# Gates of a graph network by seven half-array products over pairs of batches

## The chip, the core and the metric

The kernel runs on one core of a Trainium2 chip. The metric is the device time of one execution in microseconds (us). PE is TensorE, DVE VectorE, ACT ScalarE, POOL GpSimd; SP is SyncE, which here only issues DMA transfers.

## The reference

There are 16 batches of 1024 nodes with 128 features, and one 1024 x 1024 matrix `adj`, all float32. Layer 0 is `x = layernorm(x + adj (x W) + b)`. Layer 1 is a gated recurrence of five steps, with `adj` for both of its matrices, then again `layernorm(x + h)`:

```
m  = adj @ h;  av = concat([m, m])
u3 = h @ u3_w.T + u3_b
z  = sigmoid(av @ w3_w.T + w3_b + u3)
r  = sigmoid(av @ w4_w.T + w4_b + u3)
hv = tanh(av @ w5_w.T + w5_b + (r * h) @ u5_w.T + u5_b)
h  = (1 - z) * h + z * hv
```

As both halves of `av` are equal, the kernel adds the two halves of each `w` once and works with 128 x 128 matrices.

## The kernel before

**Work units.** Batches go in quads: four quads, five steps each, 20 steps. A tile called `rows` holds nodes on partitions (the form that the aggregation needs), a tile `hid` holds features on partitions (the form that the gates need). `agg` holds the aggregate of the quad, features on partitions, one batch to a slice.

**The aggregation** (`aggregate`, L417) is a two-level Strassen scheme in Winograd's form: seven products of half the size in the place of eight, on two levels. The seven outer products are computed in four chains, "12", "3", "67" and "54", each with an inner scheme of seven products (`chain`, L358). The right operands are sums of blocks of `rows`: `outer_sums` (L342) writes the outer ones to `tsum`, `inner_sums` (L315) the inner ones to `inner`. Chain 12 reads batches 0 and 1 of the quad only; chain 3 reads the second column half of batches 2 and 3; chains 67 and 54 read `tsum`, which takes both halves of all. Each product ends in a PSUM bank (`pa`, `pb`, `pc`), and a copy on ACT or an addition on DVE takes it on. The adjacency matrix's sums are made once.

**The gates.** The work of a step is cut into eight units, a batch and a half of its nodes (512 columns) each. A unit has five full products: `u3` (`gate_first`, L498), `w4` added to it for r (`gate_r`, L515), `w3` added to an ACT copy of it for z (`gate_z`, L531), then `w5` and `u5` in one bank (`update_products`, L539). `update_half` (L548) is tanh on ACT and a subtraction, a product and an addition on DVE. PE's order is written out by hand with `in_order`, so that a unit's `u3` stands well ahead of its other products. The first three units' `u3` products (`gates_begin`) stand between two steps.

**Back to rows.** A finished batch (for batch 3 each half) is turned in blocks of 32 x 32 on DVE (`turn_rows`, L577), written to a scratch tensor in DRAM by one transfer and read back by four (`fetch_rows`, L590), all in SP's queue in program order. The last step of a quad writes to `closing` instead, and the next quad's rows come from `saved`, which holds layer 0's result. The closing of a finished quad (`close`, `layernorm`) is spread over the next quad's steps. The very last step has an order of its own (`ending`).

**Order.** Where the text says nothing, a planner with its own costs picks the order of an engine's instructions; `keep_in_program_order` (also `in_order`) pins an instruction behind the one before it on its engine, `issue_after` queues one behind another, and hooks place work between the products of a chain.

## Time and profile before

| | |
|---|---|
| median of 3 runs | 1768.46 us (1768.37 to 1768.57) |
| the profiled execution, in all | 1769.02 us |
| its span, first to last instruction | 1766.9 us |
| busy: PE, DVE, ACT, POOL | 99%, 74%, 45%, 6% of the span |
| from one step to the next (u3 products at 448.57 and 525.21) | 76.64 us |

A profile is of one execution. The span lies between the first and the last instruction; the rest is around it. In the groups of instructions a line gives the source line, engine, operation, result and operands, shape and count, then the busy time, the mean of one in ns, and the idle time of the engine before them. In the timeline a line gives start and length in us; a float32 product is two PE instructions, whose recorded lengths overlap, so that what a product takes of PE is read from start to start. Of the DMA issues, the last column is the median time from issue to landing.

### The profile page before, as it was taken

The page shows a single profiled execution, that of the slowest core. Times are in us where ns is not written, and L with a number is a line of the kernel's source. Part 1 is how long each engine was busy: PE and PEld are TensorE (multiplying, and loading weights), DVE is VectorE, ACT ScalarE, POOL GpSimd, SP SyncE. Part 2 cuts the span into 40 slices and gives each one's busy share as a digit, 9 for nine tenths or more (in the row PEclk, how much of TensorE's full clock was granted, in tenths as well). Part 3 has the DMA queues.
Part 4 walks back from the last instruction along what each step waited for, and adds up shares of the span by engine and source line. Part 5 has one row for each costly group of instructions (what it writes and reads, how often), then busy time and mean ns, then how long its engine had stood idle before and what let it go on. Part 6 is the DMA issues. An engine that isn't in the chain of part 4 may idle for free.

```text
span 1766.9 us, 19951 instructions
## 1 busy us (share of the span) xinstructions
PE 1755.7 (99%) x6709; PEld 1265.8 (72%) x6709; DVE 1301.9 (74%) x2286; ACT 800.0 (45%) x1424; POOL 103.3 (6%) x152
## 2 busy tenths in 40 slices
PE   9999999999999999999999999999999999999998
PEld 8988885766858577685867758586675857668584
DVE  7977777676766847777778667777778577777778
ACT  4355565334353434435354452535445353443537
POOL 1202220000000000000000000000000000000004
PEclk9999999999999999999999999999999999999999
DMA  8144354051423505143351424324243241514232
GB/s 276 49 143 144 120 137 107 20 119 26 94 60 72 143 12 133 46 120 68 87 131 56 112 57 99 85 71 119 55 113 99 57 93 27 131 25 107 60 84 95
DMA packets 405332, 161.34 MB, mean 91 GB/s; under 512 B 388336, under 2 KB 389488, under 8 KB 405232
## 3 DMA queue, kind: packets, MB, share of 16 engines
q1 hardware_dynamic: 402960, 153.01, 34.3%
q0 software_dynamic: 1696, 5.24, 1.1%
q10 hardware_dynamic: 576, 1.84, 0.3%
q8 instruction: 53, 0.87, 0.2%
q14 instruction: 47, 0.39, 0.1%
HBM read 93.98 MB, written 65.01 MB: 90 GB/s over the span
## 4 chain that ended last, share of the span: by engine, by line
PE 98%; DMA 1%; DVE 0%; POOL 0%; ACT 0%; issue 0%; POOLq 0%; SPq 0%; DVEq 0%; ACTq 0%
PE pb L398 25%; PE pc L398 14%; PE pa L398 14%; PE pu L519 8%; PE ph L542 8%; PE pu L501 8%; PE ph L543 8%; PE seeded L534 8%; PE pc_x L398 3%; PE pa_x L398 3%; PE seeded L475 2%; DMA hid<-in_adj_dram 1%; DMA agg<-in_adj_dram 0%; PE pt L633 0%; PE pt_end L836 0%; POOL rstd L265 0%
## 5 line engine op out<-in xcount | busy, mean ns | idle before, releaser
L398 PE MATMUL pb<-e,inner 128*128 128x256 f32 x864 | 206.2, 379 | 0.2 <-ACT pb L382 0.2
L558 DVE TENSOR_TENSOR tsum<-tsum,hid 128x512 f32<-128x512 f32 x158 | 108.7, 688 | 106.4 <-ACT tsum L553 106.3
L553 ACT ACTIVATE tsum<-ph,bh 128x512 f32<-128x512 f32 x158 | 108.5, 687 | 164.6 <-PE ph L543 164.5
L398 PEld LDWEIGHTS pb<-e,inner 128*128 128x128 f32 x864 | 167.7, 194 | 19.2 <-ACT pb L382 0.6
L519 PE MATMUL pu<-agg,w_t 128*128 128x512 f32 x320 | 163.7, 593 | 0.0
L542 PE MATMUL ph<-agg,w_t 128*128 128x512 f32 x320 | 163.4, 592 | 0.0
L543 PE MATMUL ph<-tsum,u_t 128*128 128x512 f32 x320 | 163.4, 592 | 0.0
L534 PE MATMUL seeded<-agg,w_t 128*128 128x512 f32 x320 | 163.4, 592 | 0.0
L501 PE MATMUL pu<-hid,u_t 128*128 128x512 f32 x320 | 157.0, 592 | 0.0
L522 ACT ACTIVATE tsum<-pu,br 128x512 f32<-128x512 f32 x160 | 110.1, 688 | 85.6 <-PE pu L519 85.6
L398 PE MATMUL pb<-s,inner 128*128 128x256 f32 x576 | 148.5, 380 | 0.0
L398 PE MATMUL pb<-a,inner 128*128 128x256 f32 x576 | 143.9, 379 | 0.0
L529 DVE TENSOR_TENSOR tsum<-tsum,hid 128x512 f32<-128x512 f32 x160 | 110.1, 688 | 37.9 <-ACT tsum L522 37.9
L398 PE MATMUL pc<-e,inner 128*128 128x256 f32 x560 | 133.9, 379 | 0.0
L398 PEld LDWEIGHTS pb<-s,inner 128*128 128x128 f32 x576 | 110.5, 194 | 24.8 <-issue 10.4
L537 ACT ACTIVATE tsum<-seeded,bz 128x512 f32<-128x512 f32 x160 | 110.0, 688 | 29.3 <-PE seeded L534 29.3
L398 PEld LDWEIGHTS pb<-a,inner 128*128 128x128 f32 x576 | 111.9, 194 | 12.4
L398 PEld LDWEIGHTS pc<-e,inner 128*128 128x128 f32 x560 | 109.2, 195 | 12.8 <-PE pu L501 0.7
L543 PEld LDWEIGHTS ph<-tsum,u_t 128*128 128x128 f32 x320 | 60.8, 190 | 76.5 <-issue 59.6
L542 PEld LDWEIGHTS ph<-agg,w_t 128*128 128x128 f32 x320 | 60.6, 190 | 75.1 <-issue 74.4
L501 PEld LDWEIGHTS pu<-hid,u_t 128*128 128x128 f32 x320 | 60.8, 190 | 73.5 <-issue 72.2
L559 DVE TENSOR_TENSOR tsum<-tsum 128x512 f32<-128x512 f32 x158 | 109.1, 691 | 4.9
(192 smaller groups left out, 2854.2 us busy)
## 6 DMA issues: line engine op xcount, KB each, us to landing
turned<-ypad SPq DMA_DIRECT2D x48, 512.0 KB, 3.8
rows<-turned SPq DMA_DIRECT2D x192, 128.0 KB, 2.9
hvs<-saved SPq DMA_DIRECT2D x24, 512.0 KB, 4.1
rows<-saved SPq DMA_DIRECT2D x20, 512.0 KB, 3.7
hid<-hidden SPq DMA_DIRECT2D x64, 128.0 KB, 3.4
turned<-ypad SPq DMA_DIRECT2D x32, 256.0 KB, 2.9
rows<-turned SPq DMA_DIRECT2D x128, 64.0 KB, 2.1
hidden<-ypad SPq DMA_DIRECT2D x12, 512.0 KB, 4.1
```

Of the source, the lines that this page charges most:

```text
L398: product = nc.tensor.matmul(bank_of[a][:, ts(o, QT)], chunk(a, o, c), left[n][a][:, c, :], start=(a in (1, 5) and o == 0 and c == 0), sto ...
L501: in_order(nc.tensor.matmul(pu, w_t["u3"], hid[:, k, ts(h, HALF)], start=True, stop=True, skip_group_check=True))
L519: in_order(nc.tensor.matmul(pu, w_t["w4"], agg[:, k, cols], start=False, stop=True, skip_group_check=True))
L522: pin(nc.scalar.activation(rh[:, cols], pu, AF.Sigmoid, bias=br))
L529: pin(nc.vector.tensor_mul(rh[:, cols], rh[:, cols], hid[:, k, cols]))
L534: in_order(nc.tensor.matmul(pz, w_t["w3"], agg[:, k, cols], start=False, stop=True, skip_group_check=True))
L537: pin(nc.scalar.activation(z_of[k % 2][:, cols], pz, AF.Sigmoid, bias=bz))
L542: in_order(nc.tensor.matmul(ph, w_t["w5"], agg[:, k, cols], start=True, stop=False))
L543: in_order(nc.tensor.matmul(ph, w_t["u5"], rh_of[k % 2][:, cols], start=False, stop=True))
L553: pin(nc.scalar.activation(hv, ph, AF.Tanh, bias=bh))
L558: pinned(nc.vector.tensor_sub(hv, hv, hid[:, k, cols]))
L559: pinned(nc.vector.tensor_mul(hv, hv, z_of[k % 2][:, cols]))
```

## The change

For all steps but the very last, z and r of a pair of batches are computed as one 2 x 2 block product, [r; z] = [w4; w3] times the aggregate: the blocks of the left are w4 and w3 cut at 64 input features, those of the right are the aggregate cut at 64 features and at half of the nodes. Winograd's form takes seven block products for the eight. Each block product contracts over 64 partitions, and two batches lie side by side: batch e of the pair on partitions 64e to 64e + 63 of `agg`, in a bank of its own. For that, `rows` is kept by pairs: slice 2p + f holds feature half f of both batches of pair p, so that the aggregation gives `agg` in that form. Other parts:

- `w5` is applied as two half products over 64 partitions (`carry`); `u3` and `u5` stay full products over one batch. `u3` is applied to the first half of the nodes and to the difference of the halves (`steps_along`, on POOL), which seeds the banks of the scheme.
- The scheme's right sums are made on DVE for pair 0 and on POOL for pair 1 (`gate_sums`); its running sums are kept in two banks, with ACT copies and DVE additions in between (`gate_product`).
- The subtraction in the update moves from DVE to POOL (`update`).
- Order of a step: gates of pair 0, its u5 products and update, its turning and fetching; seeds and gates of pair 1, its u5 products and update; the next step's chain 12 follows at once. Pair 1's two halves are turned and fetched one after the other, second half of the nodes first.
- Turning writes two transfers of 64 partitions where it was one of 128; both slices of a pair wait for both batches.
- The rows of a new quad are loaded by eight transfers with pieces of 256 bytes (`load_pairs`) in the place of four.
- Weights are kept in `split`, each cut at 64 features and doubled over both partition halves; `whole_weights` puts whole ones together again for the very last step. Room for this comes out of `e12`; two left blocks are first put in `hvs` and copied to their place (`settle_left_12`).

```diff
-            tc.keep_in_program_order(nc.tensor.transpose(pt[:, :P], raw[:, :D], ident))
-            nc.vector.tensor_copy(w_t[name], pt[:, :P])
...
+            for f in range(2):
+                tc.keep_in_program_order(
+                    nc.tensor.transpose(pt[:, ts(f, P)], raw[:, ts(f, P)], ident)
+                )
+            i = SPLIT[name]
+            nc.vector.tensor_copy(
+                split[:, i : i + 2], pt[:, : 2 * P].rearrange("p (f d) -> p f d", f=2)
+            )
+        left_sums(*(split[:, i] for i in (0, 1, 2, 3, 6, 7, 8, 9)))
...
+        sums = gate_sums(0, nc.vector) if pairs else iter(())
         for dst, a, b in ((0, p7, p4), (1, p7, p4), (2, p7, p5), (3, p7, p5)):
             cols = ts(dst % 2, HALF)
             nc.vector.tensor_add(agg[:, dst, HALF:], a[:, cols], b[:, cols])
-            if dst >= 2:
+            if dst == 0:
+                next(sums, None)
+            elif dst == 1:
+                deque(sums, 0)
+            else:
                 nc.vector.tensor_add(agg[:, dst, :HALF], agg[:, dst, :HALF], p5[:, cols])
+        if pairs:
+            deque(gate_sums(1, nc.gpsimd), 0)
...
+    def steps_along(p):
+        for e in range(2):
+            h = hid[:, 2 * p + e]
+            nc.gpsimd.tensor_sub(steps_of_h[:, 2 * p + e], h[:, side(p, 1)], h[:, side(p, 0)])
+
+    def seed_pair(tag, p, role):
+        for e, t in enumerate(take(tag, p, role)):
+            k = 2 * p + e
+            h = hid[:, k, side(p, 0)] if role == "pa" else steps_of_h[:, k]
+            in_order(nc.tensor.matmul(
+                t, w_t["u3"], h, start=True, stop=True, skip_group_check=True
+            ))
...
+    def gate_product(tag, p, a):
+        n1, n2 = side(p, 0), side(p, 1)
+        right = {1: agg[:, 2 * p, n1], 2: agg[:, 2 * p + 1, n1], 3: agg[:, 2 * p + 1, n2]}
+        right.update({a: gate_right[p][:, i] for i, a in enumerate((5, 6, 7, 4))})
+        role = {1: "pa", 2: "pa", 5: "pc", 3: "pc"}.get(a, "pb")
+        for e in range(2):
+            at = ts(e, 64)
+            in_order(nc.tensor.matmul(
+                held[p, role][e], gate_left[a][at], right[a][at], start=False, stop=True,
+                skip_group_check=True,
+            ))
+        if a == 1:
+            take(tag, p, "pb")
+        for e in range(2):
+            pa, pb_, pc = (held[p, i][e] for i in ("pa", "pb", "pc"))
+            z, r = z_to[p][e], r_to[p][e]
+            if a == 1:
+                nc.scalar.copy(pb_, pa)
+            elif a == 5:
+                nc.scalar.copy(z[:, n2], pc)
+            elif a == 6:
+                nc.scalar.copy(r[:, n2], pb_)
+            elif a == 2:
+                nc.scalar.activation(r[:, n1], pa, AF.Sigmoid, bias=br)
+                times_h(p, e, n1)
+            elif a == 3:
+                nc.vector.tensor_add(r[:, n2], pc, r[:, n2])
+                nc.scalar.activation(r[:, n2], r[:, n2], AF.Sigmoid, bias=br)
+                times_h(p, e, n2)
+            elif a == 7:
+                nc.vector.tensor_add(z[:, n2], pb_, z[:, n2])
+                nc.scalar.activation(z[:, n2], z[:, n2], AF.Sigmoid, bias=bz)
+            else:
+                nc.scalar.activation(z[:, n1], pb_, AF.Sigmoid, bias=bz)
+
+    def carry(tag, p, j):
+        to = take(tag, p, f"ph{j}")
+        for f in range(2):
+            for e in range(2):
+                at = ts(e, 64)
+                in_order(nc.tensor.matmul(
+                    to[e], split[at, SPLIT["w5"] + f], agg[at, 2 * p + f, side(p, j)],
+                    start=(f == 0), stop=True, skip_group_check=True,
+                ))
+
+    def gates_of_pair(tag, p):
+        for a in (1, "n1", 2, 5, 6, 3, 7, "n2", 4):
+            if a in ("n1", "n2"):
+                carry(tag, p, int(a[1]) - 1)
+            else:
+                gate_product(tag, p, a)
...
+    def update(p, j, e, put=lambda op: op):
+        cols, k = side(p, j), 2 * p + e
+        hv = rh_of[e][:, cols]
+        nc.scalar.activation(hv, held[p, f"ph{j}"][e], AF.Tanh, bias=bh)
+        nc.gpsimd.tensor_sub(hv, hv, hid[:, k, cols])
+        put(nc.vector.tensor_mul(hv, hv, z_to[p][e][:, cols]))
+        put(nc.vector.tensor_add(hid[:, k, cols], hid[:, k, cols], hv))
...
+        if paired:
+            p, e = divmod(k, 2)
+            moves = [(between(2 * p + f, h)[:, ts(e, 64)], t[ts(f, 64)]) for f in range(2)]
+        else:
+            moves = [(between(k, h) if to is None else to, t)]
+        for to, t in moves:
+            tc.keep_in_program_order(nc.sync.dma_start(to.rearrange("g p x -> p g x"), t))
...
+    def load_pairs(q):
+        for p in range(2):
+            for f in range(2):
+                dst = rows[:, 2 * p + f].rearrange("p (c e x) -> p c e x", c=C, e=2)
+                for e in range(2):
+                    src = saved[q * QUAD + 2 * p + e].rearrange("p (c f x) -> p c f x", c=C, f=2)
+                    nc.sync.dma_start(dst[:, :, e], src[:, :, f])
...
-            for u in range(3, 8):
-                gate_first(tag, u, (u - 3) % 3)
-                step_update(u - 3, (u - 2) % 3)
-                gate_r(u - 1)
-                gate_z(u - 1)
...
-            gates_begin(then, 2 if q == NQ - 1 and s == STEPS - 2 else 3)
...
+            hooks[54][5] = [call(steps_along, 0), call(steps_along, 1)]
+            hooks[54][3, (0,)] = [call(seed_pair, tag, 0, "pa")]
+            hooks[54][4] = [call(seed_pair, tag, 0, "pc")]
+            aggregate(tag, rows, hooks, s > 0, True)
...
+            gates_of_pair(tag, 0)
+            for j in range(2):
+                reset_products(0, j)
+                for e in range(2):
+                    update(0, j, e)
+            for k in range(2):
...
+                    turn_rows(k, None, None, not final)
             if not last:
-                fetch_rows(3, 1)
-                fetch_rows(3, 0)
+                for k in range(2):
+                    fetch_rows(k)
+            seed_pair(tag, 1, "pa")
+            seed_pair(tag, 1, "pc")
+            gates_of_pair(tag, 1)
...
+                sums = first_sums(rows)
+                for j in range(2):
+                    reset_products(1, j)
+                in_order(next(sums))
+                for j, h in enumerate(SIDES[1]):
+                    for e in range(2):
+                        update(1, j, e, in_order)
+                    in_order(next(sums))
+                    for k in (2, 3):
+                        in_order(turn_rows(k, h, None, not final))
+                    for k in (2, 3):
+                        fetch_rows(k, h)
+                in_order(next(sums))
```

## The prediction

> **What bounds the kernel now.** I read the page first. Its chain of work is nearly all PE, and the clock row is 9 in every slice.

> ```profile
> span 1766.9 us, 19951 instructions
> PE 1755.7 (99%) x6709; PEld 1265.8 (72%) x6709; DVE 1301.9 (74%) x2286; ACT 800.0 (45%) x1424; POOL 103.3 (6%) x152
> PE 98%; DMA 1%; DVE 0%; POOL 0%; ACT 0%; issue 0%; POOLq 0%; SPq 0%; DVEq 0%; ACTq 0%
> ```

> PE never waits, so anything taken off PE is gained, and any wait put in front of PE is lost. Then the chain of work in order of time, for the period of a step:

> ```profile
> 448.57 2.58 PE pu L501 x6
> 525.21 2.58 PE pu L501 x6
> ```

> Each line is the three u3 products that open a step (two instructions each): one 512-column product takes 2.58/3 = 0.86 us of PE, and a step 525.21 - 448.57 = 76.64 us. That is 40 gate products (40 x 0.86 = 34.4) plus 98 aggregation products of 256 columns at 0.43. Last the timeline between two steps, engine by engine, because the change rebuilds this stretch:

> ```profile
> 525.05 2.74 PE L501 MATMUL pu<-hid,u_t 128*128 128x512 f32 x6
> 527.62 1.89 PE L398 MATMUL pa<-a,rows 128*128 128x256 f32 x8
> 539.71 1.03 PE L398 MATMUL pa<-s,rows 128*128 128x256 f32 x4
> 544.89 0.59 PE L398 MATMUL pa<-s,tsum 128*128 128x256 f32 x2
> ...
> 531.90 0.71 DVE L581 STREAM_TRANSPOSE ypad<-hid 128x512 f32<-128x512 f32 x1
> 541.51 1.22 DVE L348 TENSOR_TENSOR tsum<-tsum,rows 128x1024 f32<-128x1024 f32 x1
> ...
> 532.64 0.38 SPq L585 DMA_DIRECT2D turned<-ypad  x1
> 533.12 4.08 SPq L596 DMA_DIRECT2D rows<-turned  x8
> ```

> The last gate product ends at 525.05. Chain 12 (batches 0 and 1 only) begins at 527.62, chain 3 (batches 2 and 3, second half) at 539.71, chain 67 (tsum, from both halves of batches 2 and 3) at 544.89. The last transpose is at 531.9, SP's last eight fetches end at 537.2, and the sums that chain 67 reads (L348) end at 542.7: **2.2 us ahead of need**. The price of a transfer is in the page's DMA issues:

> ```profile
> turned<-ypad SPq DMA_DIRECT2D x32, 256.0 KB, 2.9
> rows<-turned SPq DMA_DIRECT2D x128, 64.0 KB, 2.1
> ```

> SP needs 4.08/8 = 0.51 us to issue a fetch and 0.38 plus a gap, 0.42, a write.

> [...] every product of before uses 128 rows, and PE never idles. [...] two L529 took 1.34 us from 1750.08, no longer than elsewhere, under POOL's L814 (1.61 us from 1750.95). So I price POOL's 512-wide subtraction at L814's mean, 1608 ns, with no lock.

> **The change, part by part** (19 steps; the very last keeps the old gates).

> 1. *PE's products.* Per step, 16 products by w4 and w3 become 7 per pair of batches, two half-array products in the place of one: 14 x 0.86. The w5 products become twice as many halves in the same 8 places; u3 and u5 stay 8 and 8. Saved: 2 x 0.86 = 1.72 us a step, **32.7 us** in 19. The halves are not shown in before: at best 0.86 a place, at worst 1.72 (the rival below). I take 0.86. Each pair enters and leaves the half-array mode once; a drain is unknown, between 0 and one half-product's 0.43, and I take 0.1: 0.4 a step.

> 2. *Gate phase, pair 0.* ACT's copies go from 8 to 12 a step (about 0.58 each), tanh and sigmoids stay 24. DVE keeps 32 (8 additions of r and z come, 8 subtractions go to POOL) and gets four sums, L455's 0.60 us apart. From 0.9 us after chain 54's product 4 (its copy), DVE has eleven aggregate operations and sums, then eight of r and z: 0.9 + 19 x 0.60 = 12.3 us. The seventh product, which needs the last z addition off its bank, is due at 0.86 + 0.1 + 10 x 0.86 = 9.6. Late: **2.8 us**. Before, L529 had idle time here, and only ACT's sigmoid emptied a bank. *Pair 1*: products 3 and 7 wait for two sigmoids and four copies in ACT's queue (2 x 0.69 + 4 x 0.5 after product 2, against 3 x 0.86 of PE): about 0.7; the seventh waits again for the z addition behind r's: about 0.8. With the drains **4.7 us a step**; bounds 0.4 (another order of DVE's queue) and 8.

> 3. *Rows of pair 0.* Counted from the end of product 4: POOL's four sums for pair 1 run 7.5 to 14.0, its four subtractions 15.0 to 21.4, multiplication and addition (1.44) to 22.9, transpose (1.25) to 24.1; writes land at about 27.7, eight fetches (0.52 each, 2.9 to land) at 34.3. Pair 1's last product ends at 34.8 (22 half places 18.9, 12 full 10.3, the waits above 4.7, 0.9 for chain 54's rest). So chain 12's rows, well ahead before, are just in time: I take 0.8 us late, bounds 0 and 3.

> 4. *Rows of pair 1: the deciding step.* Let T be the end of the last product, where chain 12 starts; the three u3 products (2.58 us) that used to stand between are now in chain 54. Batches 2 and 3 are now both unfinished at T, in two halves, with all their turns behind them. First half: tanh of both by T - 0.8, POOL to T + 1.5, DVE's product and addition to 3.0, the pinned sum to 3.6, two transposes to 4.9. Each transpose is now two writes: the last starts at 5.3 and lands at 7.8 (2.5, below the 2.9 of 256 KB). SP then issues eight fetches, to 12.0; they land by 13.6. The second half's transposes are long done (9.6), but its writes stand behind those fetches in SP's order: 12.0 to 13.7, landed 15.8; eight fetches to 20.0, landed 21.6; tsum's two operations 1.22 each: **24.0**. Chain 67 is due at 12.1 + 6.05 = **18.15**. PE waits 5.9 us. Chain 3's earlier wait and chain 12's (its sums stand behind the updates on DVE) lie inside that and are not added. With step 3's 0.8 and the pinned sum behind it: **6.9 us**, bounds 2 and 10. It falls in the 16 steps in which rows go on to another step; the three that change quads take rows loaded early and pay only part 2.

> 5. *Once, or hidden.* Eight 256 KB loads instead of four of 512 KB lie behind a whole gate phase, except at the first quad; six small transposes instead of three, their copies and sums, the two copies that settle the left blocks, six ACT copies at the last hand-over: 1.5 us together, bounds 0 and 6. If the gate phase stopped covering the loads it would cost up to 4 us at each of three changes.

> Sum: 16 x (6.9 + 4.7 - 1.72) = 158; 3 x (4.7 - 1.72) = 9; 1.5. The profiled execution took 1769.0 (span 1766.9 and 2.1 around it), 0.5 over the median of the runs shown: 1769.0 + 168.5 - 0.5 = **1937 us**. [...]

> **Rivals.**
> - *The waits are covered: faster.* If DVE's queue serves bank-emptying additions first and the second half's rows come by T + 18, only part 1 is left: 1769 - 32.7 + 7.6 of drains = 1744. It decides at a boundary wait under 32.7/16 = 2.0 us a step with an unhindered gate phase. For it speak PE's lack of any wait before; against it the slack of 2.2, while SP gets six more writes (2.5), four more fetches (2.1) and one more landing (2.5) in a row. Chance 0.09.
> - *The halves take turns.* Then 22 places a step cost 0.86 more: 19 x (18.9 - 1.72) = 327, the gate phase's waits vanish, the boundary's stay at 5.9 x 16 = 94: 2190. Nothing in before speaks on it[...]. Chance 0.10.
> - *Only the boundary counts*, at 4 us, the gate phase near 1.5: 16 x (5.5 - 1.7) = 60, so 1829; 1790 to 1870. Chance 0.18.
> - My forecast: 0.62, by itself 1870 to 2060. Within 0.2% of before, which is about what a measurement of this kernel can tell from no change: 0.01.

> The range 1790 to 2070 takes in the forecast and the third rival and leaves out the other cases, 0.20. Faster 0.09, same 0.01, slower 0.90.

> **What would show it.** PE's busy share falls to about 90%; waits of PE's loads for tsum (L347, L348) appear, 5 to 8 us, some 16 times; SP shows 4 writes, 8 fetches, 4 writes, 8 fetches in the boundary; POOL is busy about 590 us (19 x 16 x 1.61 and before's 103); DVE about 1355, ACT about 850; two half products start 0.43 apart and a pair's place is 0.86. Wrong I am if PE's waits are under 2 us a step, or if the seven products take 1.72 each.

## The result, and the profile after

The changed kernel takes **2204.43 us** (median of 4 runs, 2202.84 to 2210.68) against 1768.41 before: a ratio of 1.2472 (95% interval 1.2448 to 1.2497). Slower, as predicted, but by 436 us where 168 were forecast, and above the range.

The page, with the clock row of its slices:

```profile
span 2208.9 us, 22400 instructions
PE 1967.1 (89%) x7472; PEld 1330.7 (60%) x7472; DVE 1487.9 (67%) x2388; ACT 821.2 (37%) x1508; POOL 587.4 (27%) x456
PEclk9999989999999999999998999998999999989999
```

PE is busy for longer than before (1755.7) with less to do, and the clock row has eights now. PE's waits (engine, line, tile, what ended the wait: total us, times, longest):

```profile
PE pa L430 <- DVE tsum L380: 71.0, 16, 6.1
PE pb L668 <- DVE tsum L691: 51.0, 28, 6.5
PE pb L430 <- DVE inner L350: 32.5, 16, 2.6
PE pc L430 <- DVE inner L349: 28.5, 24, 2.0
PE pa L430 <- DMA rows<-turned: 11.1, 10, 1.6
```

In this kernel L430 is the aggregation product, L668 the half-products of a gate product; L380 makes `tsum`, L349 and L350 are inner sums, L691 is the z addition. The first line is chain 67 at the boundary, 16 times, as predicted. The second is the gate phase of pair 0. The third is chain 12 waiting for its own sums; the fourth is the same in 14 cases and in 10 chain 3 waiting for its.

To see where 436 us went I split PE's time, from its first product to its last, in four. **Work** is the number of products times their start-to-start distance at full clock (0.43 us for an instruction of 512 columns over 128 rows, from 2.58 us for six in the kernel before; 0.216 for 256, from 1.73 us for eight there; half of 0.43 for one of two halves that run side by side, from 1.72 us for eight below). **Idle** is time in which no product runs. **Clock** is busy time multiplied by the share of the clock that was not granted in it. **Rest** is what remains. All four are worked out from the trace of the profiled execution (2210.68 us for the changed kernel); only the runs below test what they mean.

| kernel | work | idle | clock | rest |
|---|---|---|---|---|
| before | 1750.5 | 2.8 | 0.0 | 3.5 |
| changed | 1718.2 | 270.7 | 126.9 | 83.4 |

The idle time is 73.5 us at chain 67 by this count, 67.5 at the inner sums of chain 12 (53.7) and chain 3 (13.8), 69.3 at the z additions (56.5 of pair 0, 12.8 of pair 1), 11.8 at landing rows (nearly all at chain 3), and smaller waits.

Now one step, whose chain 12 starts at T = 612.73. First PE in the gate phase before it (timeline: start, length, engine, line; then the idle time ahead in brackets):

```profile
572.67 0.59 PE L430 MATMUL pc<-e,tsum 128*128 128x256 f32 x2
573.19 1.13 PE L668 MATMUL pa<-agg,split 64*128 64x512 f32 x4
574.15 1.88 PE L701 MATMUL ph<-agg,split 64*128 64x512 f32 x8
575.87 1.02 PE L668 MATMUL pa<-agg,split 64*128 64x512 f32 x4
...
584.65 3.75 PE L668 MATMUL pb<-first,split 64*128 64x512 f32 x4 [1.63 <-DVE tsum L691]
588.32 5.50 PE L715 MATMUL ph<-tsum,u_t 128*128 128x512 f32 x8
593.67 1.88 PE L653 MATMUL seeded<-hid,u_t 128*128 128x512 f32 x4
```

Eight half-array instructions (L701) take 575.87 - 574.15 = 1.72 us: 0.86 for a place of two half-products. So the halves run side by side here. But after a wait, eight full-array instructions (L715) take 593.67 - 588.32 = 5.35 us instead of 3.44. The table of stretches shows why; its columns after the stretch are its length, each engine's busy time and count (PE, PE's loads, DVE, ACT, POOL), then PE's granted clock, the DMA share and GB/s:

```profile
566.20:573.19 6.99, 6.99 (x25) 4.47 (x23) 0.83 (x2) 0.59 (x1) 0.00 (x0) 1.00 0.00 0
573.19:593.67 20.48, 18.66 (x54) 7.52 (x54) 14.02 (x21) 10.33 (x17) 10.01 (x6) 0.83 0.01 1
629.14:641.50 12.36, 5.60 (x25) 4.42 (x23) 3.89 (x6) 2.06 (x5) 0.00 (x0) 0.93 0.58 134
641.50:653.00 11.50, 11.27 (x41) 9.77 (x42) 11.50 (x14) 2.70 (x5) 3.02 (x2) 0.78 0.20 46
```

What goes ahead of such a stretch can be counted in the changed kernel's trace. I cut its time at full clock into pieces of that grid, each ending 0.15 us before a point of it (the first 40 us are left out), and counted in each, from the recorded lengths, the share in which PE's array was in use, a half-array product that runs alone as half. Of 553 pieces 52 have half the clock behind them, with shares of at most 0.48; the 501 others have at least 0.46. Ahead of 585.2 the share was 0.41, though PE stood still for only about 1.6 us: a half ran alone beside the wait. Ahead of 619.3 it was 0.50, and the clock stayed. This is a count in one trace, which no run was made to test.

Then the boundary: SP's queue, and on DVE what it serves:

```profile
620.37 2.63 SPq L748 DMA_DIRECT2D turned<-ypad  x4
624.28 4.17 SPq L757 DMA_DIRECT2D rows<-turned  x8
628.55 2.65 SPq L748 DMA_DIRECT2D turned<-ypad  x4
632.48 4.73 SPq L757 DMA_DIRECT2D rows<-turned  x8
```

```profile
614.29 1.09 DVE L349 TENSOR_TENSOR inner<-rows 128x512 f32<-128x512 f32 x1 [6.21 <-DMA rows<-turned]
615.31 1.75 DVE L725 TENSOR_TENSOR tsum<-tsum,agg 128x512 f32<-128x512 f32 x1
...
639.10 1.23 DVE L379 TENSOR_TENSOR tsum<-rows 128x1024 f32<-128x1024 f32 x1 [7.07 <-DMA rows<-turned]
640.36 1.23 DVE L380 TENSOR_TENSOR tsum<-tsum,rows 128x1024 f32<-128x1024 f32 x1
```

Four writes, eight fetches, four writes, eight fetches: the predicted row. Pair 0's rows come at 614.29, T + 1.6, and the first of chain 12's sums (L349), pinned ahead of pair 1's update, holds DVE's product L725 back until then; and that product takes 1.75 us where such a product took 0.69 before.

### The profile page after: what moved, and what is told of

Read it like the earlier page. It is cut to its first block, busy times and chain, and to the rows that moved or that the text cites. A ratio compares the mean times of both kernels' runs of the same rounds, so it can differ in the third digit from the quotient of the medians.

```text
span 2208.9 us, 22400 instructions
## 1 busy us (share of the span) xinstructions
PE 1967.1 (89%) x7472; PEld 1330.7 (60%) x7472; DVE 1487.9 (67%) x2388; ACT 821.2 (37%) x1508; POOL 587.4 (27%) x456
## 5 line engine op out<-in xcount | busy, mean ns | idle before, releaser
L724 POOL TENSOR_TENSOR tsum<-tsum,hid 128x512 f32<-128x512 f32 x152 | 218.0, 1458 | 376.1 <-ACT tsum L723 375.8
L647 POOL TENSOR_TENSOR inner<-hid 128x512 f32<-128x512 f32 x76 | 116.6, 1538 | 630.5 <-PE pc L430 516.4
L430 PE MATMUL pb<-e,inner 128*128 128x256 f32 x672 | 177.4, 408 | 36.0 <-DVE inner L350 32.5
L430 PE MATMUL pb<-a,inner 128*128 128x256 f32 x760 | 189.8, 383 | 11.9 <-DVE first L418 8.5
L430 PEld LDWEIGHTS pb<-e,inner 128*128 128x128 f32 x672 | 139.1, 209 | 60.8 <-issue 14.2
L430 PE MATMUL pc<-e,inner 128*128 128x256 f32 x560 | 146.2, 403 | 28.7 <-DVE inner L349 28.5
L430 PEld LDWEIGHTS pb<-a,inner 128*128 128x128 f32 x760 | 147.2, 195 | 33.2 <-DVE first L418 9.7
L430 PE MATMUL pb<-s,inner 128*128 128x256 f32 x576 | 162.6, 408 | 4.4 <-DVE rows L418 3.0
L725 DVE TENSOR_TENSOR tsum<-tsum 128x512 f32<-128x512 f32 x76 | 91.0, 1217 | 111.7 <-POOL tsum L724 111.7
L430 PE MATMUL pa<-s,tsum 128*128 128x256 f32 x320 | 97.4, 422 | 71.0 <-DVE tsum L380 71.0
L668 PE MATMUL pb<-first,split 64*128 64x512 f32 x228 | 110.0, 720 | 51.4 <-DVE tsum L691 51.0
L430 PEld LDWEIGHTS pc<-e,inner 128*128 128x128 f32 x560 | 113.3, 207 | 51.9 <-DVE inner L349 21.9
L430 PEld LDWEIGHTS pb<-s,inner 128*128 128x128 f32 x576 | 119.0, 209 | 32.8 <-issue 9.5
L488 DVE TENSOR_TENSOR agg<-rows 128x512 f32<-128x512 f32 x88 | 58.9, 691 | 114.2 <-ACT rows L420 114.2
L349 DVE TENSOR_TENSOR inner<-rows 128x512 f32<-128x512 f32 (+1 forms) x44 | 32.5, 739 | 152.9 <-DMA rows<-turned 142.2
L349 POOL TENSOR_TENSOR inner<-agg 128x512 f32<-128x512 f32 x19 | 61.6, 3241 | 266.3 <-ACT tsum L680 245.5
L726 DVE TENSOR_TENSOR hid<-hid,tsum 128x512 f32<-128x512 f32 x152 | 125.7, 838 | 3.0
L430 PEld LDWEIGHTS pa<-s,tsum 128*128 128x128 f32 x320 | 67.1, 215 | 84.9 <-issue 76.8
L668 PE MATMUL pb<-inner,split 64*128 64x512 f32 x266 | 109.6, 626 | 9.1 <-DVE agg L691 8.4
L701 PE MATMUL ph<-agg,split 64*128 64x512 f32 x456 | 116.8, 591 | 0.0
L715 PE MATMUL ph<-tsum,u_t 128*128 128x512 f32 x152 | 106.4, 865 | 0.0
## 6 DMA issues: line engine op xcount, KB each, us to landing
turned<-ypad SPq DMA_DIRECT2D x64, 256.0 KB, 4.0
rows<-saved SPq DMA_DIRECT2D x32, 256.0 KB, 3.9
```

The source lines that it names most:

```text
L349: yield engine.tensor_sub(dst[0], xs(0, 1), xs(0, 0))
L430: product = nc.tensor.matmul(bank_of[a][:, ts(o, QT)], chunk(a, o, c), left[n][a][:, c, :], start=(a in (1, 5) and o == 0 and c == 0), sto ...
L488: nc.vector.tensor_add(agg[:, dst, HALF:], a[:, cols], b[:, cols])
L647: nc.gpsimd.tensor_sub(steps_of_h[:, 2 * p + e], h[:, side(p, 1)], h[:, side(p, 0)])
L668: in_order(nc.tensor.matmul(held[p, role][e], gate_left[a][at], right[a][at], start=False, stop=True, skip_group_check=True,))
L701: in_order(nc.tensor.matmul(to[e], split[at, SPLIT["w5"] + f], agg[at, 2 * p + f, side(p, j)], start=(f == 0), stop=True, skip_group_check ...
```

## The experiments

The rivals after the result: *lock* (DVE and POOL hold each other up, so DVE's queue is late everywhere), *standing still* (waits cost twice, once as idle time and once as clock), *boundary* (the row of transfers behind pair 1). Each edit is against the changed kernel unless it says otherwise.

**1. The subtraction back on DVE.**

```diff
-        nc.gpsimd.tensor_sub(hv, hv, hid[:, k, cols])
+        put(nc.vector.tensor_sub(hv, hv, hid[:, k, cols]))
```

> The changed kernel with the update's subtraction back on DVE (pinned with the product and addition behind it); POOL keeps the sums and the steps of h. Theory lock: [...] Then the update's product and addition fall from means of 1217, 943 and 838 ns to 0.69 us, the wait for tsum between steps falls from 6.3 us to 3 to 5, and the time falls from 2204 to 2120 to 2180, although DVE has eight instructions a step more. Theory load: DVE is simply full and POOL slow, without a lock; then DVE's durations were long for another reason, DVE gets 19 x 8 x 0.6 = 91 us more, and the time is 2204 or more.

Measured 2160.57 us, ratio 1.2216 (1.2180 to 1.2251), 44 us under the changed kernel. The groups of DVE's product (L725, its two forms; count, then busy time and mean ns), first of the changed kernel, then of this one:

```profile
L725 DVE TENSOR_TENSOR tsum<-tsum 128x512 f32<-128x512 f32 x76 | 91.0, 1217 | 111.7 <-POOL tsum L724 111.7
L725 DVE TENSOR_TENSOR tsum<-tsum,agg 128x512 f32<-128x512 f32 x76 | 71.5, 943 | 12.3 <-POOL tsum L724 12.3
```

```profile
L725 DVE TENSOR_TENSOR tsum<-tsum,agg 128x512 f32<-128x512 f32 x76 | 52.5, 691 | 2.3
L725 DVE TENSOR_TENSOR tsum<-tsum 128x512 f32<-128x512 f32 x76 | 52.1, 686 | 0.6
```

DVE got 152 more instructions and its busy time hardly moved (1487.9 to 1496.8): POOL had taken nothing off it. So the time and the means fit theory lock; its forecast that the wait for `tsum` shrinks fails, as chain 67's wait stays (80.3 against 73.5). The lost clock falls by 35.4 us and the idle time by 16.0, while the rest rises by 2.6; together this is the 48.7 us by which the profiled execution is shorter. How much of it is the lock and how much that a subtraction takes 1.46 us on POOL and 0.68 on DVE, this run does not tell apart.

**2. In the kernel before, only the subtraction to POOL.**

```diff
-        pinned(nc.vector.tensor_sub(hv, hv, hid[:, k, cols]))
+        nc.gpsimd.tensor_sub(hv, hv, hid[:, k, cols])
```

> The kernel before with one part of the change alone: the update's subtraction on POOL instead of DVE. Theory lock: DVE's product and addition of the update and r times h stretch from 0.69 us to 0.9 to 1.6 when they meet a subtraction, some sums too, and PE begins to wait: 1780 to 1880. Theory no lock: DVE's durations stay at 0.69 us and only the end of a step is about 1 us later, within the slack of 2.2 us: 1768 to 1775.

Measured 1778.27 us, ratio 1.0053 (1.0030 to 1.0076). In between: L559's mean rose from 691 to 776 ns, L560's from 685 to 724, but PE idles only 10.7 us, most of it (6.6) in the ending, where half the clock behind it costs another 2.9. Between the steps, where the work has slack, the longer operations cost PE next to nothing; it is the changed kernel's tight queue that pays.

**3. All of POOL's 512-wide work on DVE** (the subtraction, `gate_sums(1)`, `steps_along`).

> The changed kernel with all of POOL's 512-wide work on DVE: subtractions, the steps of h and pair 1's sums, 16 instructions a step. Theory lock: every DVE duration returns to its value of before (0.69 us), so that DVE's busy time stays within 5% of the present 1488 us although it has 304 instructions more, and the time falls to 2080 to 2170. Theory load: DVE becomes the bound of the gate phase and the time rises above 2204.

Measured 2177.71 us, ratio 1.2312 (1.2270 to 1.2355). DVE is busy 1519.3 us with 304 more instructions, every such operation 0.68 to 0.69: the lock again. But the time lies between the two intervals, it is no faster than experiment 1, and pair 0's z wait is 71.5: the lock is not all that makes the z additions late.

**4. Without pair 1's rows between the steps of a quad.**

```diff
-                    for k in (2, 3):
-                        in_order(turn_rows(k, h, None, not final))
-                    for k in (2, 3):
-                        fetch_rows(k, h)
```

> The changed kernel without the turning, writing and fetching of pair 1's rows between two steps of a quad (the aggregation then reads old rows of batches 2 and 3). Theory boundary: the transfers' wait ahead of chain 3 (1.0) and chain 67 (6.3) and the half clock behind it (2.9) go, about 10 us in 16 steps: 2204 falls to 2030 to 2070; chain 12's waits for its sums (4 us) shrink by the 1.3 us of two transposes or stay. Rival theory, that the gate phase and DVE's load are the main cost and would take the time back: above 2130.

Measured 2063.63 us, ratio 1.1668 (1.1606 to 1.1729). The turning, writing and fetching of pair 1 cost 141 us of the 436, 8.8 in each of 16 steps, with the clock they cost in it (idle 175.6, clock 72.3).

**5. Filler in the boundary's wait**: six products to no purpose ahead of chain 3's last product, in 15 steps (the very last, which has an order of its own, gets none).

```diff
+            if s > 0:
+                hooks.setdefault(3, {}).setdefault(4, []).insert(0, call(fill, tag))
```

> The changed kernel with six more products of 512 columns (5.2 us of PE, into a free bank that nobody reads) ahead of the last product of chain 3 in 16 steps, that is inside PE's wait for chain 67. Theory clock: PE's clock is halved because PE stands still for 6 us; the filler keeps it up, so although PE gets 16 x 5.2 = 83 us of work more, the half clock behind the wait (2 to 3 us a step) goes and the time falls from 2204 to 2150 to 2180. Rival: the half clock has another cause (the gate phase, the half-array products), the filler only fits into the wait: 2202 to 2215.

Measured 2220.31 us (2214.58 to 2226.05), ratio 1.2556 (1.2479 to 1.2633): above both intervals. The split is clearer: chain 67's wait falls from 73.5 to 6.5 us and the lost clock from 126.9 to 97.9; in 15 of the 16 steps of the changed kernel half the clock stood at chain 67's start (10) or set in within 1.4 us of it (5), and here none follows the filler in 15 steps. Standing still does cost clock, some 29 us here, but 77.2 us of extra work replaced 67 of wait, and 23 of idle time came up elsewhere.

**6. Three orders of the same work**, each with the subtraction on DVE. The first traces pair 1's aggregate additions and sums behind pair 0's gates; the second gives pair 1's second half its w5 and u5 products ahead of the last gate product, so that it can be updated earlier, and puts pair 0's first seeds into the boundary's wait; the third has both.

```diff
+            rest_of_pairs(rows)          # first: behind gates_of_pair(tag, 0)
...
-        for a in (1, "n1", 2, 5, 6, 3, 7, "n2", 4):
+        early = (1, "n1", 2, 5, 6, 3, "n2", 7, "r2", 4, "r1")
+        for a in early if p else (1, "n1", 2, 5, 6, 3, 7, "n2", 4):
...
-            hooks[54][3, (0,)] = [call(seed_pair, tag, 0, "pa")]
+            if s > 0:
+                hooks.setdefault(3, {}).setdefault(4, []).insert(0, call(seed_pair, tag, 0, "pa"))
```

> The kernel with the subtraction on DVE (2160.6 us), and with the four additions that make pair 1's aggregate, and pair 1's sums behind them, issued after pair 0's gate products instead of ahead of them. Theory of the gate phase: pair 0's seventh product waits because DVE works through pair 1's aggregate first; 4 x 0.6 = 2.4 us of it go, the wait of PE for the z addition (59.7 us in all) falls under 20 us, its half clock goes too: 2070 to 2120. Rival: DVE is the bound of the gate phase, so that the wait turns up again in pair 1 (its sums are later): 2145 to 2165.

> The kernel with the subtraction on DVE (2160.6 us), and with two things for the stretch between steps: pair 1's second node half gets its u5 products before the seventh product, so that it is updated, turned and fetched first and earlier; and the next step's two u3 seeds of the first half stand ahead of chain 3's last product instead of in chain 54 (1.7 us of PE put into the wait). Theory boundary: the wait for chain 67 (80 us in 16 steps) falls by 1.7 + 1 to 1.7 us a step, some half clock with it: 2085 to 2125. Rival: SP's row of 24 transfers is the whole of it and starts no earlier: only the seeds count, 2130 to 2145.

> Both of the last two together. Theory: the two waits are separate, so both gains add up, and with shorter waits the clock is halved less often: 2000 to 2070. Rival: they trade against each other on DVE: not more than 20 us below the better one of the two.

Measured 2160.35, 2134.99 and 2131.59 us; ratios 1.2217 (1.2133 to 1.2301), 1.2074 (1.2038 to 1.2109), 1.2054 (1.2019 to 1.2089). The first moved nothing, and its trace says why: the planner still ran the additions ahead of the r and z operations, so its theory was not tried, though the time lies in the rival's interval. The second gains 26 us over experiment 1, as its rival has it: chain 67's wait falls from 80 to 58.9 and the rest from 86.0 to 68.8, although PE now changes between whole and half products six times a step instead of four. The third adds nothing sure (its rival again).

**7. The z additions truly first.** Now an explicit edge puts r*h, pair 1's aggregate additions and its sums behind the z additions on DVE.

```diff
+                z_added[0] = nc.vector.tensor_add(z[:, n2], pb_, z[:, n2])
...
+        if a == 7:
+            with tc.issue_after(z_added[0].ins):
+                for e in range(2):
+                    times_h(p, e, n1)
+                    times_h(p, e, n2)
...
+            with tc.issue_after(z_added[0].ins):
+                rest_of_pairs(rows)
```

In the three kernels of this part the loads of a new quad stand ahead of the moved additions, so in the three steps that change quads these read the new quad's rows.

> The subtraction is back on DVE (2160.6 us by itself), and now DVE is made to serve the additions that empty PE's banks first: the z additions stand directly behind the r additions, and the products r*h, the last four aggregate additions and POOL's sums of pair 1 come only after them. Theory (pair 0's z additions are late because of what stands ahead of them on DVE): their wait falls from 60 us to under 15, and some 15 to 25 us of lost clock go with it: 2075 to 2105 us. Rival (the wait only moves to what is now behind: r*h in front of the u5 products, POOL's sums in front of pair 1's products): 2135 to 2165.

> The same for pair 0, with the other order of pair 1 and the later seeds (2135.0 us by themselves). Theory: the gains add up, 2050 to 2085 us. Rival (the boundary's wait takes back what the gate phase gives, as its end is set by the chain from pair 1's last product): 2110 to 2140. Faster than before, 1768: not expected by either.

> The z additions first, and between the steps of a quad the rows of pair 1 are not turned, written and fetched (their update is still made), so that the chains read old rows for batches 2 and 3. Theory: the waits of the boundary (141 us, from the kernel that leaves out only this) and of the gate phase (60 to 85) are separate and add up: 1930 to 1975 us, with the clock lost while PE is busy under 55 us. Rival (with the boundary gone, the gate phase's wait was already smaller, or PE stands still elsewhere): 2010 to 2050, clock lost still about 70.

Measured 2148.20 (ratio 1.2153, 1.2124 to 1.2182), 2117.53 (1.1970, 1.1952 to 1.1988) and 1990.33 us (1.1260, 1.1241 to 1.1279). The theories missed; the rivals have the first two, and the third lies between the two. The wait of pair 0 is gone and has come up again in pair 1. Groups of the gate products into `pb`, pair 0's (`first`) and pair 1's (`inner`), of the changed kernel, then of the first of these (L678 and L699 are its product and z addition):

```profile
L668 PE MATMUL pb<-first,split 64*128 64x512 f32 x228 | 110.0, 720 | 51.4 <-DVE tsum L691 51.0 <-DVE first L350 0.2
L668 PE MATMUL pb<-inner,split 64*128 64x512 f32 x266 | 109.6, 626 | 9.1 <-DVE agg L691 8.4
```

```profile
L678 PE MATMUL pb<-inner,split 64*128 64x512 f32 x266 | 101.2, 645 | 45.0 <-DVE agg L699 45.0
L678 PE MATMUL pb<-first,split 64*128 64x512 f32 x228 | 78.6, 606 | 0.0
```

And the timeline of the same kernel says who moved it: DVE with pair 0's update, and POOL with pair 1's sums, in the same microseconds.

```profile
578.29 0.69 DVE L737 TENSOR_TENSOR tsum<-tsum,hid 128x512 f32<-128x512 f32 x1
579.01 1.64 DVE L738 TENSOR_TENSOR tsum<-tsum 128x512 f32<-128x512 f32 x1
580.57 1.75 DVE L737 TENSOR_TENSOR tsum<-tsum,hid 128x512 f32<-128x512 f32 x1
582.25 1.75 DVE L739 TENSOR_TENSOR hid<-hid,tsum 128x512 f32<-128x512 f32 x1
583.92 1.75 DVE L738 TENSOR_TENSOR tsum<-tsum 128x512 f32<-128x512 f32 x1
585.60 0.68 DVE L737 TENSOR_TENSOR tsum<-tsum,hid 128x512 f32<-128x512 f32 x1
```

```profile
577.34 2.76 POOL L349 TENSOR_TENSOR inner<-agg 128x512 f32<-128x512 f32 x1 [27.12 <-DVE agg L503]
580.18 1.59 POOL L350 TENSOR_TENSOR inner<-agg,inner 128x512 f32<-128x512 f32 x1
581.74 1.71 POOL L351 TENSOR_TENSOR inner<-agg 128x512 f32<-128x512 f32 x1
583.41 1.71 POOL L352 TENSOR_TENSOR inner<-agg,inner 128x512 f32<-128x512 f32 x1
```

Beside POOL's first sum, which takes 2.76 us, DVE's operation of 578.29 still takes 0.69: there the long one is POOL's. From 579.01 on DVE's operations start 1.56 to 1.68 us apart, one for each of POOL's; as soon as POOL is through (585.12), they take 0.68 again and start 0.60 apart.

**8. The same without the lock there:** pair 1's sums on DVE, behind the moved additions, and the loads of a new quad behind both. The second leaves out pair 1's rows again, the third puts pair 0's first seeds into the boundary's wait (as in part 6).

```diff
-        deque(gate_sums(1, nc.gpsimd), 0)
+        deque(gate_sums(1, nc.vector), 0)
```

> As the kernel with the z additions first (2148.2 us), but POOL's four sums for pair 1 are made on DVE, behind the last aggregate additions, and the loads of a new quad stand behind those additions. In the kernel with the z additions first, pair 0's wait went and 48 us came up at pair 1's z additions, as DVE's updates of pair 0 took 1.64 to 1.75 us each under POOL's sums and 0.68 behind them. Theory (the lock moved the wait): without POOL there, pair 1's wait falls under 20 us: 2095 to 2125 us. Rival (DVE has too much to do in the gate phase, whoever makes the sums): the wait stays at 40 or more: 2140 to 2160.

> The same, and between the steps of a quad the rows of pair 1 are not turned, written and fetched (the chains read old rows for batches 2 and 3). Theory (waits of gate phase and boundary, and the clock they cost, are the whole of the loss): 1920 to 1965 us, idle time under 110 and lost clock under 50. Rival: 1980 to 2000, as the kernel before it without these rows (1990.3).

> The first of these kernels, with pair 0's first seeds ahead of chain 3's last product (in the boundary's wait) instead of in chain 54, where a step follows another of its quad. Theory (work put in the wait shortens it and keeps the clock): 25 to 45 us under the first kernel, chain 67's wait near 45. Rival (the seeds there cost as much as they cover): within 10 us of it.

Measured 2103.95 (ratio 1.1897, 1.1880 to 1.1915), 1947.75 (1.1016, 1.0995 to 1.1036) and 2074.62 us (1.1736, 1.1717 to 1.1756): all three in the theory's interval. The first changes two things, the sums' engine and the loads' place; the latter bears on the three steps that change quads, and these became 10.6 us shorter, of the 38.8 by which the profiled execution is shorter. Both gate phases now flow:

```profile
L678 PE MATMUL pb<-inner,split 64*128 64x512 f32 x266 | 99.4, 619 | 10.4 <-DVE agg L699 10.4
L678 PE MATMUL pb<-first,split 64*128 64x512 f32 x228 | 78.7, 606 | 0.0
```

| kernel | idle | clock | rest | total |
|---|---|---|---|---|
| changed | 270.7 | 126.9 | 83.4 | 2204.4 |
| 1: subtraction on DVE | 254.7 | 91.5 | 86.0 | 2160.6 |
| 7: z additions first | 277.7 | 75.2 | 60.7 | 2148.2 |
| 8: no lock there | 259.9 | 51.8 | 63.2 | 2104.0 |
| 8, seeds in the wait | 234.9 | 43.2 | 64.3 | 2074.6 |
| 8, without pair 1's rows | 140.8 | 11.4 | 62.3 | 1947.8 |

Work is 1718.2 in each. The parts are those of the profiled execution, between PE's first and last product; the total is the median of the runs, so the parts do not add up to it. The lost clock falls from 126.9 to 11.4 us as the waits go, though no edit touches the clock itself. The last line had one miss: its idle time was to be under 110 and is 140.8. Some 75 of that are pair 0's rows and chain 12's sums, which stay without pair 1's rows and which wait more (26.3 for pair 0's rows, 0.9 in the changed kernel) now that PE arrives earlier. The third kernel of part 8 is the best version found, 130 us under the changed kernel; it does not reach the kernel before.

## Why the prediction was right and wrong

**Right: step 1.** 32.7 us of PE were to be saved, on an estimate of 0.86 us for a place of two halves that no product of before showed; the work falls by 1750.5 - 1718.2 = 32.3, a count of products; what the trace measures is that a place of two half-products takes 0.86 us (574.15 to 575.87). That refutes the rival in which the halves take turns, although its 2190 us lies nearer to the result than the forecast: a total can agree by the wrong road.

**Right in kind: steps 3 and 4.** Rows of pair 0 came about a microsecond or two late, and SP's row of transfers sets the sums for chain 67, whose wait was 6.12 us in the step shown and 71.0/16 = 4.4 on average, against 5.9. Chain 67's due time was put 0.9 us too late: by the prediction's own lines it is 544.89 - 527.62 = 17.27, not 18.15, as chain 67's first product stands ahead of chain 3's last. Wrong was the sentence that chain 12's and chain 3's waits lie inside that one and are not added. Chain 12's are 53.7/16 = 3.4 a step and chain 3's, with its rows, about 1.5. They delay chain 67's need, but the sums came later too (T + 28.8 instead of T + 24.0), since the late rows of pair 0 hold the pinned sum, that holds DVE's product, and so pair 1's transposes and SP's writes: its first began at T + 7.6, where the forecast had the last at T + 5.3. Two steps that I had priced apart stand in one queue.

**Right in size, wrong in cause: step 2.** Gate waits were put at 4.7 a step with 0.4 of drains; the z additions' idle time is 69.3/19 = 3.6, with 3.0 at pair 0 (2.8 forecast) and 0.7 at pair 1 (1.5). The cause was to be the count of DVE's operations alone. Putting the z additions first (part 7) emptied pair 0's wait, which supports the count; that it came up again in pair 1 and went with POOL's sums (part 8) shows the lock as the other half.

**Wrong: the price of POOL's work.** The forecast adds nothing for what DVE and POOL cost each other, because "two L529" took 1.34 us under POOL. The lines say otherwise:

```profile
1750.08 1.34 DVE L529 TENSOR_TENSOR tsum<-tsum,hid 128x512 f32<-128x512 f32 x1 [0.35 <-ACT tsum L522]
```

```profile
1749.27 1.60 POOL L813 TENSOR_TENSOR inner<-tsum,hid 128x512 f32<-128x512 f32 x1 [0.77 <-ACT tsum L537]
1750.95 1.61 POOL L814 TENSOR_TENSOR inner<-hid,inner 128x512 f32<-128x512 f32 x1
```

The count at the end is x1: one operation took 1.34 us, the longest of 160 with a mean of 0.69, and it ran from under L813 into L814. So the trace of before showed a price of 1.34 - 0.69 = 0.65 us for one meeting. Under POOL's sums 0.69 became 1.75 us (part 7), and in the changed kernel means became 1217 and 943 ns. Experiment 1 prices the subtraction's move at 44 us, experiments 7 and 8 the sums' at about as much again, with the loads' place in it.

**Wrong: the clock, put at nothing.** This is the largest miss: the forecast's sum has no term for a slower clock, and 126.9 us of busy time were lost to it. That the clock stays full behind a wait was an assumption: before, PE idled 2.8 us in all, and its clock row is 9 in every slice. In the changed kernel half the clock followed not only the boundary's wait of 6.12 us but also a wait of 1.63 us with halves running alone, ahead of 585.2. So the gate phase pays as well as the boundary. Experiment 5 and part 8 show that the waits are the cause: with them the lost clock goes, to 11.4 us. What a wait costs in clock was to be had only from a trace with waits.

**Wrong: the three steps that change quads "pay only part 2".** PE's waits in the gate phase of one of them:

```profile
688.31 3.27 PE L668 MATMUL pb<-first,split 64*128 64x512 f32 x4 [5.71 <-DVE tsum L691]
713.32 2.78 PE L668 MATMUL pb<-inner,split 64*128 64x512 f32 x4 [3.51 <-DVE agg L691]
```

```profile
683.71 1.07 DVE L349 TENSOR_TENSOR inner<-rows 128x512 f32<-128x512 f32 x1 [3.16 <-POOL inner L350]
```

The rows are there early, so the next step's first sum (L349) stands in DVE's queue in the middle of the gate phase, ahead of the r and z additions. DVE stands idle for 3.16 us before it, until one of POOL's sums for pair 1 is through. Such a step takes 107.9 us from chain 12 to chain 12 and the next 89.7, together as much as two others of 99.

**Too small: the drains, and what else is in the rest.** 7.6 us of drains were forecast; the rest is 83.4 against 3.5. The traces show two parts of it.

- *Changes of mode.* From whole to half products, the first half product starts 573.19 - 572.67 = 0.52 us behind two instructions that take 0.43 elsewhere, and its place takes 574.15 - 573.19 = 0.96 us instead of 0.86. That is 0.19 us a change where 0.1 was forecast. On the way back it is the same (a last half product at 608.67, the full ones behind it at 609.19 and, one place on, 610.16), and 15 us in the 76 changes of the 19 steps; a part of this was counted as idle time.
- *Halves out of step.* When only one of two banks is emptied, one half runs alone. That is so for 136 us in the changed kernel's trace; side by side, and at full clock, the same products would have taken 58 us less. In the 14 kernels that have the half-array products, the rest goes from 49 to 86 us; less what the lone halves cost it stays at 24 to 31. So they are the part that the order of the work moves (down to 35 us in part 8). No run was made for this alone, and some 10 to 20 us of the rest stay open.

In sum, against the profiled execution (2210.68 us): waits 267.9 more than before instead of 193.6, clock 126.9 instead of 0, rest 79.9 instead of 7.6. These are 74 + 127 + 72 = 273 of the 274 us that were missed. In the forecast's terms, the steps that failed are the clock put at nothing, the waits of chains 12 and 3 taken to lie inside chain 67's (67.5 + 11.8 us, where 0.8 a step was taken), the drains, and behind the gate phase and the boundary alike the price of POOL's work without a lock.

## What to carry to other kernels

When TensorE, which never waited, is given waits, count the slow clock behind them as well: here 127 us beside 268 of new waits. Before moving work to an engine that can hold up the busy one, look for a stretch in which both run, and compare the length of one operation there with its length elsewhere (here 1.75 us against 0.69). Read the count at the end of the line with it: one long operation was taken for two short ones here. Operations that empty a bank for the bound engine go first in their queue by an explicit edge: where the others were only traced later (part 6), the planner still put them ahead.

## What the runs showed that was not expected

- In part 7's stretch DVE and POOL take turns, one operation for one, at about 1.67 us a pair, where DVE's alone start 0.60 us apart.
- The same move, of the subtraction to POOL, cost 10 us in the kernel before (experiment 2), nearly all in its ending, and 44 in the changed one (experiment 1): its price is that of the queue behind it.
- Work put into a wait kept the clock: the filler took 29 us off the loss. Useful seeds in the same place gave 2103.95 - 2074.62 = 29.3 us in all, most of it idle time (25.0) and 8.6 of it clock.
- Half the clock did not follow idle stretches alone: in the changed kernel's trace it stood behind pieces of 3.41 us in which the array was in use for up to 0.48.
